# A gated state-space block: from a scheduled order of units to a written order of pairs

## The chip, the core and the metric

The kernel runs on one core of a Trainium2 chip. The core has five engines that work side by side, each on its own queue of instructions and in the order of that queue: TensorE (PE in the profile; its weight loads are shown apart as PEld), VectorE (DVE), ScalarE (ACT), GpSimd (POOL) and SyncE (SP), which here only issues DMAs. Results of TensorE land in PSUM, a small memory of eight banks; everything else is kept in SBUF, and DMAs move data between SBUF and the large memory (HBM).

The metric is the time of one execution on the device in microseconds (us). All arithmetic is in 32-bit floats.

## The reference

The input is four sequences of 512 tokens with 512 channels. A small modulation first: `mod = silu(c) @ wmod` gives six vectors of 512 for every sequence (shift, scale and gate, twice). Then

- `h = layernorm(x) * (1 + ca) + sa`, and a Mamba-2 layer on `h`: a projection to 3136 columns (1024 of x, 512 of B, 512 of C, 1024 of z, 64 of dt), a causal convolution of four taps and silu on x, B and C, `dt = softplus(...)`, the chunked scan below, a skip term, a product with `silu(z)` and a projection back to 512 columns;
- `x = x + ga * that`, a second layer norm with its own shift and scale, a 512 x 512 product with binarized weights (sign times mean size) and a bias, and `x = x + gb * that`.

The scan has 64 heads of 16 channels; eight heads share one group of B and C (64 states). In chunks of 128 tokens:

```
A_cum        = cumsum(-dt) inside the chunk
Lm[s, z]     = exp(A_cum[s] - A_cum[z])    for z <= s, else 0
Y_diag[s]    = sum_z  (C[s] . B[z]) * Lm[s, z] * X[z]
states[c+1]  = states[c] * exp(A_cum[end]) + sum_z B[z] * exp(A_cum[end] - A_cum[z]) * X[z]
Y_off[s]     = (C[s] . states[c]) * exp(A_cum[s])
y            = Y_diag + Y_off + D * X / dt
```

## The kernel before

The 2048 tokens are worked on in eight **halves** of 256 tokens (`T`), two to a sequence, each with two chunks of 128. The groups are taken two at a time (`gp`, four of them). A **unit** is one chunk of one half and one `gp`, that is 16 heads; there are 64 units, eight to a half.

For each half there is a **front**: load and layer norm (`f_norm`), transposes on TensorE and modulation into `hT` (`f_hT`), dt and its cumulative sums (`f_dt`, which writes the sums to HBM, `sums_d`, so that they can be read back repeated over 128 partitions), the tiles of 128 projected columns (`f_B`, `f_C`, `f_x` through `conv_pair`, and `f_z`; the products are `proj`, L432 to 434), and transposes of x and B to token order (`f_xt`, `f_Bt`). A convolved tile needs one ACT instruction (L450) and three DVE instructions (L454), a pair of tiles one tanh (L458) and one last DVE product (L459).

For each unit there are three stages. `stage0` loads the sums into two `decay` tiles of 128 x 8 x 128 (L541 and L542) and, except in a sequence's first chunk, the tile `e`. `stage1` masks C.B (`gm`, L621), takes eight exponentials for each decay tile on ACT (`exps`, L549) and multiplies each tile by `gm` on DVE (L625). `stage2` makes the 16 **strip** products `py` (TensorE, 32 columns of its array each, four of them side by side; L212 and L215), gathers the output on DVE and POOL (L666 to L675), and feeds the states (`new_states`). `burst` (L598) makes the products of C with B and with the states for two units at a time in the bank `gy`. There are four decay tiles, so two units have their tiles at once; for the last units, free parts of the weights `win` are used as well.

For each chunk a **tail** follows: the output projection `po` (L739), gates, layer norm, transposes `ph`, modulation `h`, the product `pf` (L775) and the store of `o`.

The order in which each engine gets its instructions isn't the order in which the Python code runs. The tables `FRONT`, `FIRST` and `SECOND` give the steps at which parts are traced, and the scheduler of the tile framework then orders the instructions from their priorities and its own estimates. The kernel bends that order in places: `glued` keeps a row of products together and places it behind the newest projection (`tc.issue_after`), `behind` places a front's later part behind the half's newest projection, `first_dt` raises the priority. Early in the run one queue, SP, carries all loads in turn: the inputs, `win`, then `load_late` (4 MB of modulation weights that borrow the place of `wout` and `bwT`), later `wout` itself (2 MB, `load_wout`) and the four 256 KB tiles `fw` of the second layer's weights (`signs`, L272, summed by DVE in L274). PSUM has five banks for everything in rotation (tag `mm`), two for `gy`, one for `py`.

Of the kernel before, what the change touches and what calls it, by code (L numbers as in the profile page):

```python
# [2 lines left out]

# [8 lines left out]
F32 = mybir.dt.float32  # L12
# [24 lines left out]
SERIES = [0.11612164612, 0.108532879004, 0.142961789972, 0.19999853166, 0.333333336603]  # L37


@with_exitstack  # L40
def adaln_mamba_block(
# [31 lines left out]
    xs_of = {}  # L73

    def load_x(h, queue=nc.sync):
# [5 lines left out]
        xs_of[h] = tiles  # L81


    ct = keep.tile([P, NK, B], F32, name="ct")
    nc.sync.dma_start(ct, cT)
    load_x(0, nc.scalar)


    ident = keep.tile([P, P], F32, name="ident")
    make_identity(nc, ident)  # L90
    ones = keep.tile([P, P], F32, name="ones")
    nc.gpsimd.memset(ones, 1.0)

    upto = keep.tile([P, P], F32, name="upto")
    nc.gpsimd.affine_select(
        out=upto, in_=ones, compare_op=ALU.is_ge, fill=0.0, base=0,
        pattern=[[1, P]], channel_multiplier=-1,
    )
    mhalf = keep.tile([P, 2], F32, name="mhalf")
    nc.gpsimd.memset(mhalf, -0.5)  # L100


    NXP = 4
    xpads = []
    for i in range(NXP):
        xp = keep.tile([P, 2, 2 * HPG * 2 * HD], F32, name=f"xpad{i}")
        xpads.append(xp)

    NE = 4
    decays = []  # L110
    for i in range(NE):
        et = keep.tile([P, HPG, CH], F32, name=f"decay{i}")
        decays.append(et)

    win = keep.tile([P, NK, PROJ], F32, name="win")
    wout = keep.tile([P, NKI, DM], F32, name="wout")
    bwT = keep.tile([P, NK, DM], F32, name="bwT")
    modT = keep.tile([P, 4, NK, B], F32, name="modT")
    gate_d = dram.tile([B, 3, DM], F32, name="gate_d")
    sums_d = dram.tile([NHALF, 2, NH, CH], F32, name="sums_d")  # L120
    e_d = dram.tile([NHALF, 2, NH, CH], F32, name="e_d")
    r_d = dram.tile([NHALF, NH, 2, CH], F32, name="r_d")

    w_in_v = w_inT.rearrange("(k p) e -> p k e", p=P)

    def load_win(lo, hi, after=None):
        d = nc.sync.dma_start(win[:, :, lo:hi], w_in_v[:, :, lo:hi])
        if after is not None:

            tc.add_manual_dep(  # L130
                d.ins, after, mybir.DependencyInfo(mybir.DependencyClass.Sync, mybir.DependencyReason.DATA)
            )
        return d.ins
# [772 lines left out]
```

## Time and profile before

| | |
|---|---|
| time, median of three executions | 737.01 us (735.02 to 738.54) |
| span of the profiled execution | 735.7 us |
| instructions | 15007 |
| TensorE busy | 700.4 us (95%) |
| VectorE busy | 599.5 us (81%) |
| ScalarE busy | 522.0 us (71%) |
| GpSimd busy | 254.8 us (35%) |
| moved by DMA | 99.24 MB, mean 135 GB/s |

The profiled execution's own time is not given apart from its span; the span lies 1.3 us below the median of the three timed executions. A line of a group reads: line, engine, operation, tile written and tiles read, shapes, how often, and behind the bar the busy time in us and the mean of one in ns, then the idle time of the engine before these instructions and what ended it. A matmul of 32-bit floats shows as two records, a transpose as one. Matmuls are pipelined: a record's duration is longer than the distance from one start to the next, and the distance is what a product costs in a row of them. In the chain of waits (the work that ended last, followed back from the end) and in the timeline, a line has start, length and what, all in us from the start of the span.

Two half-periods of the steady part: the strips of the first unit of halves 2, 3, 4, 5, 6 and 7 start at 248.4, 336.0, 421.7, 509.3, 595.0 and 682.7 us, some 86.9 us apart. Half 1 starts at 162.4 us.

### The profile page before, as it was taken

How to read it: one execution, taken by the hardware profiler on the slowest of the kernel's cores; microseconds unless marked ns; L12 is line 12 of the kernel's file. 1: busy time of each engine (PE TensorE's matmuls, PEld its weight loads, DVE VectorE, ACT ScalarE, POOL GpSimd, SP SyncE). 2: the span in 40 equal slices, each digit the busy share in tenths (PEclk: the TensorE clock that was granted, in tenths of full speed). 3: DMA queues.
4: the chain of work that ended last, by engine and by line, in shares of the span. 5: the costliest groups of instructions: out<-in, count | busy, mean ns of one | idle time of the engine just before them, and what ended most of it. 6: DMA issues, size and time to landing. Idle time of an engine off the chain costs nothing.

```text
span 735.7 us, 15007 instructions
## 1 busy us (share of the span) xinstructions
PE 700.4 (95%) x5196; PEld 500.8 (68%) x5196; DVE 599.5 (81%) x1170; ACT 522.0 (71%) x1507; POOL 254.8 (35%) x297
## 2 busy tenths in 40 slices
PE   6999979899999999999999999999999999999997
PEld 3786746666677666677677666776667866677754
DVE  3869888876998678986899768996799867996995
ACT  2467658748696697785976787865968768788941
POOL 4021323444243332343223342433414332333652
PEclk9999989999999999999999999999999999999999
DMA  8991693535555256444644256552564537457720
GB/s 279 328 291 41 204 208 85 135 98 142 127 132 144 63 155 137 102 115 102 159 116 130 53 116 168 142 137 53 140 132 114 130 86 176 116 150 151 142 69 29
DMA packets 119067, 99.24 MB, mean 135 GB/s; under 512 B 73984, under 2 KB 97152, under 8 KB 118992
## 3 DMA queue, kind: packets, MB, share of 16 engines
q1 hardware_dynamic: 117808, 96.39, 52.3%
q0 software_dynamic: 896, 1.38, 0.7%
q8 instruction: 41, 0.67, 0.4%
q10 hardware_dynamic: 288, 0.52, 0.2%
q14 instruction: 34, 0.28, 0.1%
HBM read 92.47 MB, written 5.79 MB: 134 GB/s over the span
## 4 chain that ended last, share of the span: by engine, by line
PE 65%; ACT 16%; DVE 9%; DMA 4%; issue 4%; POOL 1%; SPq 1%; ACTq 0%; DVEq 0%; POOLq 0%
PE po L739 14%; PE pp_x L434 11%; PE pp_z L434 10%; ACT decay L549 9%; PE pp_C L434 7%; PE pp_B L434 5%; PE pf L775 3%; PE py L212 2%; PE py L215 2%; DVE decay L625 2%; ACT h L759 2%; DVE u_x L454 2%; DMA fw<-in_ffn_w 2%; ACT win L549 2%; PE gy L215 2%
## 5 line engine op out<-in xcount | busy, mean ns | idle before, releaser
L549 ACT ACTIVATE decay<-decay,st 128x128 f32<-128x128 f32 x960 | 293.9, 395 | 4.2 <-DMA decay<-sums_d 3.7
L625 DVE SCALAR_TENSOR_TENSOR decay<-decay,gm 128x1024 f32<-128x1024 f32 x120 | 160.8, 1341 | 50.3 <-ACT decay L549 47.2
L434 PE MATMUL pp_x<-hT,win 128*128 128x259 f32 x512 | 120.7, 390 | 7.3 <-DVE u_C L454 7.3
L434 PE MATMUL pp_z<-hT,win 128*128 128x256 f32 x512 | 118.1, 383 | 0.0
L434 PEld LDWEIGHTS pp_x<-hT,win 128*128 128x128 f32 x512 | 96.9, 193 | 25.2 <-ACT decay L549 7.7
L739 PE MATMUL po<-wout,z 128*128 128x512 f32 x256 | 113.8, 595 | 0.0
L434 PEld LDWEIGHTS pp_z<-hT,win 128*128 128x128 f32 x512 | 94.3, 189 | 16.3 <-issue 3.5
L675 POOL TENSOR_TENSOR z<-yt,z 128x256 f32<-128x256 f32 x62 | 62.9, 1015 | 76.1 <-DVE yt L674 57.8
L454 DVE SCALAR_TENSOR_TENSOR u_x<-pp_x,cw,u_x 128x256 f32<-128x256 f32 x192 | 83.6, 474 | 1.3 <-ACT u_x L450 0.7
L739 PEld LDWEIGHTS po<-wout,z 128*128 128x128 f32 x256 | 47.5, 190 | 53.1 <-issue 52.4
L672 POOL TENSOR_TENSOR yt<-yt,xs 128x256 f32<-128x256 f32 x46 | 41.4, 899 | 106.3 <-DVE yt L671 78.6
L507 POOL TENSOR_TENSOR xs<-u_x,rr 128x512 f32<-128x512 f32 x32 | 42.7, 1334 | 79.2 <-DVE u_x L459 61.3
L516 ACT ACTIVATE uz<-pp_z,zb 128x256 f32<-128x256 f32 x64 | 27.5, 470 | 59.0 <-PE pp_z L434 59.0
L215 PE MATMUL py<-decay,xpad 128*32 128x128 f32 x1680 | 66.3, 276 | 0.0
L434 PE MATMUL pp_B<-hT,win 128*128 128x259 f32 x256 | 63.5, 396 | 2.7 <-ACT decay L549 1.9
L434 PE MATMUL pp_C<-hT,win 128*128 128x259 f32 x256 | 59.6, 384 | 1.1 <-DVE u_x L454 1.1
L775 PE MATMUL pf<-bwT,h 128*128 128x512 f32 (+1 forms) x136 | 59.0, 578 | 1.4 <-ACT h L759 1.3
L434 PEld LDWEIGHTS pp_B<-hT,win 128*128 128x128 f32 x256 | 47.4, 193 | 14.5 <-ACT decay L549 3.1
L450 ACT ACTIVATE u_x<-pp_x,cb,cw 128x256 f32<-128x256 f32 x64 | 35.3, 560 | 30.5 <-PE pp_x L434 30.4
L434 PEld LDWEIGHTS pp_C<-hT,win 128*128 128x128 f32 x256 | 47.8, 189 | 9.4 <-PE pn L424 1.4
L679 POOL TENSOR_TENSOR xd<-xpad,st 128x256 f32<-128x256 f32 x48 | 34.1, 727 | 55.8 <-PE pst L215 28.3
L212 PE MATMUL py<-decay,xpad 128*32 128x128 f32 x240 | 47.4, 279 | 3.2 <-issue 2.2
(157 smaller groups left out, 1080.9 us busy)
## 6 DMA issues: line engine op xcount, KB each, us to landing
decay<-sums_d SPq DMA_DIRECT2D x120, 256.0 KB
decay<-sums_d SPq DMA_DIRECT2D x120, 128.0 KB
rr<-r_d SPq DMA_DIRECT2D x64, 128.0 KB
e<-e_d SPq DMA_DIRECT2D x96, 64.0 KB
win<-in_w_inT SPq DMA_DIRECT2D x4, 1024.0 KB
xr<-in_x SPq DMA_DIRECT2D x16, 256.0 KB
res<-o SPq DMA_DIRECT2D x15, 256.0 KB
x<-in_x SPq DMA_DIRECT2D x14, 256.0 KB
```

The lines of the kernel that those rows point to most:

```text
L212: first = products[0]()
L215: product()
L434: last = mm(pm, win[:, k, col : col + P], H[h]["hT"][:, k, lo:], start=(k == 0), stop=(k == NK - 1))
L450: nc.scalar.activation(u[:, j, :], pm[:, KS - 1 :], AF.Identity, bias=cb[:, t : t + 1], scale=cw[:, t, KS - 1 : KS])
L454: nc.vector.scalar_tensor_tensor(u[:, j, :], pm[:, k : k + T], cw[:, t, k : k + 1], u[:, j, :], ALU.mult, ALU.add)
L507: nc.gpsimd.tensor_tensor(xs, xc, rr, ALU.mult)
L549: nc.scalar.activation(ets[r][:, i, :], ets[r][:, i, :], AF.Exp, bias=H[h]["st"][:, hd : hd + 1], scale=-1.0)
L625: nc.vector.scalar_tensor_tensor(ets[r], ets[r], 1.0, bc_mid(gm[:, r, :], HPG), ALU.min, ALU.mult)
L672: ew.tensor_add(t, t, xs)
L675: ew.tensor_mul(zg, t, zg)
L739: last_po = mm(po, H[h]["z"][g // 2][:, g % 2, c * CH : (c + 1) * CH], wout[:, g, :], start=(g == 0), stop=(g == NKI - 1))
L775: mm(pf, h2[:, k, :], bwT[:, k, cols], start=(k == 0), stop=(k == NK - 1))
```

## The change

Tile's scheduler is no longer asked for the order: the whole body runs inside `tc.manual_schedule()`, and each engine issues in the order in which the code traces its instructions. That order comes from a small queue. Every part of the work is a Python generator (a task) that yields the planned time of its next piece; `Plan.run` always continues the task with the smallest planned time. The planned times are in a table `PLAN`, in units of one step (eight to a half), with own rows for the first half (`@0`) and the last (`@7`). `glued`, `behind`, `first_dt` and all `issue_after` are gone.

The scan works on **pairs** of units: 32 pairs in place of 64 units. `gm`, `e`, `yt`, `py`, `z` and `xs` are tiles for a pair, so the DVE and POOL instructions on them have 512 elements in a row of a partition where they had 256, and there are half as many. The 32 strip products of a pair are traced in one block. There are six decay tiles (`ND`), four to a pair, in rotation: of the next pair's four tiles, two can be loaded before this pair's strips are done. To make room in SBUF, the scratch memory for DMA descriptors is cut to 2048 bytes (`SCRATCH`).

Smaller edits: `new_states` makes eight products of 32 columns in place of four of 64; `f_Bt` turns only the first chunk in a sequence's second half (two transposes in place of four, in four halves); the signs of the second layer's weights are made in place; `load_late` is planned at -3.55, ahead of all loads of decay tiles (-2.85 and later) and of `rr`, while before its first load stood ahead of them and the other five behind the first four decay tiles; `wout` is planned at 1.25 and the first `fw` load at 2.3.

```diff
+class Plan:
+    def at(self, t, f, *args):
+        self.push(t, f(*args))
+    def push(self, t, task):
+        heappush(self.queue, (t, self.count, task))
+        self.count += 1
+    def run(self):
+        while self.queue:
+            now, _, task = heappop(self.queue)
+            t = next(task, None)
+            if t is not None:
+                self.push(max(now, t), task)
...
+TAP = 0.04
+ND = 6
+PLAN = {
...
+    "loads": (-3.55, 1.25,),
+    "signs0": (2.3, 2.7, 1.95, 2.85, 3.25, 3.4,),
...
+    "B0": (1.15, 1.3, 1.4, 1.55, 1.75, 1.85,),
...
+    "pair1": (2.0, 0.1, 0.5, 1.2, 1.65, 2.1, 2.1, 2.35, 2.4, 2.65, 2.3, 2.35, 2.5,),
+    "decay10": (-0.95, -0.6, -0.2, 0.2,),
+    "decay11": (0.1, 1.05, 1.2, 1.6,),
...
+    "decay02@0": (-2.6, -1.8, -1.3, -0.85,),
+    "decay03@0": (-2.85, -1.5, -1.0, -0.75,),
...
-    def glued(products, after=None):
-        with tc.issue_after(after) if after else nullcontext():
-            first = products[0]()
-        with tc.issue_after(first.ins), tc.high_priority(offset=1000):
-            for product in products[1:]:
-                product()
...
+    def f_Bt(h, q, w):
+        n = 1 if h % HPB == HPB - 1 else 2
+        pt = to_tokens(H[h]["B"][q], f"bt_{h}_{q}", n)
...
+    def decayed(n, i, room, w):
+        h, c, q = of_pair(n)
...
+        et = rooms[room]
...
+        nc.sync.dma_start(et[0:mid], src.partition_broadcast(mid))
+        nc.sync.dma_start(et[mid:, :, mid:], src[:, mid:].partition_broadcast(mid))
+        for k in range(HPG):
+            yield w[1] + (w[2] - w[1]) * k / (HPG - 1)
+            hd = c * NH + head + k
+            nc.scalar.activation(et[:, k, :], et[:, k, :], AF.Exp, bias=H[h]["st"][:, hd : hd + 1], scale=-1.0)
+        yield w[3]
+        gm = gm_of[n]
+        nc.vector.scalar_tensor_tensor(et, et, 1.0, bc_mid(gm[:, i % 2, i // 2, :], HPG), ALU.min, ALU.mult)
...
+    def masked(n):
...
+        gm = wk.tile([P, 2, 2, CH], F32, tag="gm", name=f"gm_{n}", bufs=1)
+        nc.vector.tensor_mul(gm, new_of[n], upto.unsqueeze(1).unsqueeze(1).to_broadcast([P, 2, 2, CH]))
...
+    def strips(n, w):
+        h, c, q = of_pair(n)
+        py = ps.tile([P, 2, 2, CH], F32, tag="y", bufs=1, name=f"py_{n}")
+        for u in range(2):
+            xp = xp_of[h, 2 * q + u][:, c, :]
+            for r in range(2):
+                et = decay_of[n, 2 * u + r]
+                for s in range(2):
+                    for j in range(HPG // 2):
+                        lo = r * 2 * P + 32 * (2 * j + s)
+                        mm(
+                            py[32 * j : 32 * j + 32, r, u, :], xp[:, lo : lo + 32], et[:, 2 * j + s, :],
+                            start=(s == 0), stop=(s == 1),
+                        )
...
+            for j in range(4):
+                mm(pst[32 * j : 32 * j + 32, u, :], bt[:, c, u, 32 * j : 32 * j + 32],
+                   xd[:, j // 2 * P : (j // 2 + 1) * P], start=True, stop=True)
...
+                room = ND + 4 * (n % 2) + i if n >= NPAIR - 2 else (4 * n + i) % ND
+                w = planned(f"decay{p}{i}", h, now)
+                at(w[0], decayed, n, i, room, w)
...
+    with tc.manual_schedule():
+        plan.run()
...
-    nc = bacc.Bacc("TRN2", target_bir_lowering=False, num_devices=1)
+    nc = bacc.Bacc("TRN2", target_bir_lowering=False, num_devices=1, dynamic_dma_scratch_size=SCRATCH)
```

Laid out in the order of issue on TensorE, the block of strips of a pair, its `gy` burst and its `pst` products now mostly stand next to each other; before, the strips stood in 72 places and the dt products `pa` in 22, now in 32 and 8.

## The prediction

> **What bounds the kernel now.** I read the spans and busy shares first, then the chain of waits, then TensorE's own waits, then the timeline of a steady stretch.
>
> ```profile
> core 0: 735.7 us, clock 0.993
> ...
> PE 700.4 (95%) x5196; PEld 500.8 (68%) x5196; DVE 599.5 (81%) x1170; ACT 522.0 (71%) x1507; POOL 254.8 (35%) x297
> ...
> PE 65%; ACT 16%; DVE 9%; DMA 4%; issue 4%; POOL 1%; SPq 1%; ACTq 0%; DVEq 0%; POOLq 0%
> ```
>
> TensorE is the bound, but busy time says little, since pipelined records overlap. The chain of waits gives the true price of a product in a row of them:
>
> ```profile
> 357.56 3.70 PE pp_B L434 x16
> 361.27 3.51 PE pp_C L434 x16
> 364.77 6.87 PE po L739 x16
> 371.64 0.30 PE gy L212
> ```
>
> A 259-column product costs 3.51/16 = 0.219 us, a 512-column one 6.87/16 = 0.429. The first row is the same work as the second and 0.19 longer: before it TensorE stood on the narrow products `py` and `pa` and had to change to another tile of its array. The other direction is in the timeline:
>
> ```profile
> 341.00 0.60 PE L757 MATMUL ph<-ident,t 128*128 128x128 f32 x4
> 341.53 0.30 PE L212 MATMUL py<-decay,xpad 128*32 128x128 f32 x1
> ...
> 346.78 0.37 PE L212 MATMUL gy<-C,S 64*128 64x128 f32 x1
> 346.79 0.37 PE L215 MATMUL gy<-C,S 64*128 64x128 f32 x1
> 347.00 0.27 PE L212 MATMUL gy<-C,S 64*128 64x128 f32 x1
> ```
>
> Four transposes cost 4 x 0.109 = 0.44, but `py` starts 0.53 after them: 0.09 for the change. The second step of `gy` follows after 0.22 and the later ones after 0.112: 0.11 more. So a change of tile form costs 0.1 to 0.2 us; over all 247 changes in the trace the mean is 0.17.
>
> The sum of TensorE's time, then. Products in a row: 1024 x 0.219 + 512 x 0.216 (`pp_z`) + 256 x 0.429 (`po`) + 120 x 0.429 and 16 x 0.215 (`pf`) = 500; strips 512 groups of four x 0.109 = 56; `gy` 224 x 0.112 = 25; transposes 372 x 0.109 = 41; the rest (`pst`, `pa`, `pg`, `pn`) 26: together 648. Changes of form: 247 x 0.17 = 42. First product at 6.2, and 4.0 from the start of the last one to the end. What is left of 735.7 is 735.7 - 648 - 42 - 10.2 = 35.5: true waits. Where they lie:
>
> ```profile
> PE pp_x L434 <- DVE u_C L454: 7.3, 2, 5.4
> PE pg L221 <- DVE sc L197: 6.2, 1, 6.2
> PE pa L368 <- ACT hT L347: 3.3, 8, 0.6
> ```
>
> ```profile
> 83.06 13.38 DMA fw<-in_ffn_w
> ...
> 99.41 6.23 PE pp_x L434 x16
> ```
>
> ```profile
> 90.00:97.60 7.60, 3.93 (x51) 2.84 (x49) 5.80 (x17) 3.51 (x8) 4.31 (x7) 1.00 1.11 239
> 97.60:104.50 6.90, 5.09 (x12) 4.08 (x13) 6.90 (x16) 4.70 (x14) 0.95 (x2) 0.51 1.06 256
> ```
>
> The longest (5.4 us, the first row) is the `fw` load behind 2 MB of `wout`: DVE waits for it in L274, its convolution taps stand behind, five banks of PSUM fill, TensorE stops. The last table (busy time of PE, PEld, DVE, ACT, POOL, then clock) shows the price again: 6.9 us at clock 0.51, some 3.4 lost. With 1.7 lost at another half-clock stretch near 16 us and smaller gaps before 140 us, the start has 19.5 of the 35.5; the end 3.2; the steady part 12.8, about 1.9 for each half.
>
> **The change, part by part.**
>
> *Fewer changes of form.* In the written order of each kernel I count them: 247 before, 134 after (strips stand in 32 places in place of 72, `pa` in 8 in place of 22, `pst` next to narrow work). 113 x 0.17 = 19.2 off the path. Bounds: 0.09 (the entry alone) gives 10, 0.20 gives 23. I take the mean of the whole trace.
>
> *Products.* 16 transposes fewer: 16 x 0.109 = 1.7 off. `pst` has eight products of 32 columns where it had four of 64. No row shows `pst` so; side by side as `py` is (four in 0.109) they take the same two steps, one by one 96 steps more x 0.109 = 10. I take 0, since `py`, the same tile form, starts its four 7 ns apart.
>
> *DVE and POOL.* 176 DVE instructions of 256 elements (L621, L666, L671, L674; 0.41 each) become 88 of 512 (0.69, as L742): 72 - 61 = 11 less. On POOL 108 of 0.90 to 1.02 become 54 (1.33, as L507): 32 less. I cost both at nothing: TensorE covers them.
>
> *Two of four decay tiles are late.* With six tiles, two of the next pair's can be loaded only after this pair's strips. The path: load 3.9 to 5.0 (the chain's rows `decay<-sums_d`), two tiles of exponentials 2 x 2.44, one mask 1.24: about 11. In the shortest interval between two pairs TensorE has 16 `pp` products of each of two kinds (7.0), `po` (6.9), strips (1.75), `pt_bt` and `gy` (0.9), changes (0.5) = 17.0, so 15.2 after the strips. Adding each engine's rows between the same marks, DVE has 15.9 and ACT 14.5 there; in the longest interval 27.8, 23.2 and 19.8. TensorE has the most work in every steady interval, so I cost this wait at 0; without that cover it would be about 1 us a pair.
>
> *The start.* The `fw` loads are planned a step after `wout` (some 11 us), so I let the 5.4 and its 3.4 of clock go. What is late next: `load_late` now stands ahead of the first decay tiles on SP, 3.1 MB more than before. At 287 GB/s (mean of the first 60 us) that is up to 10.7 us; the first exponentials, at 46.3 before, come between 46 and 57. TensorE's written order gives it products until about 59 (16 tiles of 1.75, three z of 3.5 and 6 of small work after 16.75, less the 2 of `pa` that lie before); ACT has some 19 to do there: 40 exponentials (0.305 each, 12), eight taps and tanhs (7). If the loads land at 46 and the taps and tanhs fall beside them, the strips are ready by 59: no wait. If they land at 57 and all 19 comes after: 76, a wait of 17. I take 7, a little under the middle, because the first tile to land already feeds ACT. Start: 1.7 + 7.3 of small gaps + 7 = 16.
>
> *Order as written.* All queues are now strict as traced, and a wait at the head of ACT, DVE, POOL or SP holds what is planned behind it: exponentials hold convolution taps and so PSUM banks; on SP a store of `o` (L907) holds decay loads. POOL's own four DMAs a half stand behind its `xd` and ahead of `z`; three steps pass before `sums_d` is read. Bounds for the steady part: 0, and 25 (twice the present 12.8, from the idle of a queue that passes on its waits). Of the present ones, those of `pa` and `phT` among split strips (0.5 to 0.9 each) go; I take 10. The end keeps its chain `po`, norm, `ph`, `pf`: 4.
>
> *Sum.* 6.2 + (648 - 1.7) + 134 x 0.17 (22.8) + (16 + 10 + 4) + 4.0 = 709.3 of span. The span before lies 1.3 under its median; that gives 710.6, and I say 710.
>
> **A rule weighed.** The row: a gap of 5.4 us was followed by 6.9 us at clock 0.51; one of 2.1 us near 130 was not (clock 1.00 from 128 to 132). The Trainium skill, "TensorE: Matmul & The Clock Gate", section "HAM oscillation — how this bites in real kernels", puts the limit at gaps of about 3.4 us. By the rows a gap between 2.1 and 5.4 is undecided, and 7 would be a fall of the clock if it came in one piece; my sum assumes that it comes in several and stays at 710. By the page's limit one piece of 3.4 is enough, and with it the sum would be about 714.
> The same page, in "Architectural detail: the array is 16× 32×32, not 1× 128×128", calls the ACT and DVE queues strict first-in first-out, which speaks against a finely interleaved written order; this trace has 214 us of idle ACT and passes only a few us on to TensorE.
>
> **The rivals.**
>
> 1. *Nearly all waits vanish.* For it: TensorE has the most work in each interval. Against: the loads at the start. Waits 9 + 0 + 3 = 12: 691 + 1.3 = 692. Chance 0.20 (below 700).
> 2. *The start gets worse:* the first strips wait 17 in one piece with 3.4 of clock, and `fw` is late again (5.4): 10 + 3.4 + 5.4 = 19 over my sum: 729. For it: the DMA share is 0.93 in the first 60 us, so nothing comes early. Chance 0.17 (718 to 734).
> 3. *The change doesn't do what it says:* the time for changes of form only moves into waits for operands, 19 + 7 back: 736, within 0.5% (734 to 741). Chance 0.05.
> 4. *Slower: every pair waits for its last two decay tiles.* The place is `strips`: 32 products in one block, so `pst` and the projections stand behind the fourth mask on TensorE, where before eight strips could go with one tile. For it: ACT has 14.5 of the 17.0 us between pairs and its exponentials stand in line with taps that wait for TensorE. Against: 15.2 us of cover for 11. It decides from 1.0 us a pair (31 pairs, 31 us over my sum); at 1.6 a pair 50 more: 760. Chance 0.16.
>
> My own case (700 to 718) has 0.42. Faster by over 0.5% is 0.42 + 0.20 + 0.17 = 0.79, within 0.5% (about what a measurement of this kernel can tell from none) 0.05, slower 0.16. The range that leaves out two in ten, some 0.06 below and 0.14 above: 691 to 742.
>
> **What would show it.** Right: `pp_B` and `pp_C` in the chain mostly at 3.51; halves 82 to 84 us apart in place of 86.9; TensorE's longest waits below 5 us and before 75 us; no clock of 0.5 near 100 us. Wrong: `py` waiting for DVE `decay` or ACT in every pair (rival 4); `fw` or `decay` loads again at the start of the chain (rival 2); halves still near 87 with few waits on TensorE (the price of a change mis-sized). The forecast fails if in-order waits exceed 60 us in all.

## The result and the profile after

| | before | after |
|---|---|---|
| median time | 735.03 us (20 executions, 732.98 to 738.54) | 739.97 us (20 executions, 735.19 to 745.91) |
| ratio after to before, 95% interval | | 1.0068 [1.0047, 1.0089] |
| span of the profiled execution | 735.7 us | 742.7 us (its time is 744.44) |
| mean granted clock of TensorE | 0.993 | 0.978 |

The change makes the kernel 0.7% slower. The forecast was 710 us, with a range of 691 to 742. The profiled execution lies 4.5 us above the median of its kernel; the accounts below are made against its own span.

These lines answer to those of the prediction. The spans:

```profile
core 0: 742.7 us, clock 0.978
```

The page's busy times, and the shares of the chain that ended last:

```profile
PE 690.0 (93%) x5372; PEld 506.9 (68%) x5372; DVE 606.1 (82%) x1080; ACT 523.5 (70%) x1507; POOL 239.3 (32%) x245
...
PE 44%; DVE 22%; DMA 12%; ACT 12%; issue 5%; SPq 3%; POOL 1%; ACTq 0%; DVEq 0%; POOLq 0%
```

TensorE held 65% of that chain before and holds 44% now; DVE went from 9 to 22% and DMAs from 4 to 12%. Less of the chain is TensorE's own work, and more of it is work that TensorE waited for. Part of the chain around a pair's strips (start, length, what):

```profile
610.13 3.51 PE pp_C L563 x16
...
614.28 1.88 PE py L771 x64
616.16 0.44 PE pst L824 x16
616.60 3.65 PE pp_z L563 x16
```

`pp_C` costs 3.51 here, since it stands behind `pp_B` of the same form; `pp_z` behind the narrow `pst` costs 3.65 for 16 x 0.216 = 3.46, a change of 0.19. All strips of a pair stand in one block of 1.88 us. `pst` takes 0.44 for its 16 records, 0.027 each, like the strips: the eight narrower products cost nothing more, as was assumed.

TensorE's largest groups of waits, from the list of what each engine waited for (us in total, times, longest); the row left out (`pg`, 6.5 us at the very start) has its like in the kernel before:

```profile
PE ph L885 <- DVE t L437: 12.2, 2, 8.4
PE py L771 <- ACT decay L707: 7.3, 4, 3.0
...
PE py L771 <- DVE decay L710: 4.4, 2, 2.4
PE pt_bt L621 <- DVE B L572: 3.9, 5, 1.5
PE gy L717 <- DVE C L572: 3.4, 1, 3.4
```

**Where the time is, by stage.** For each stage I take TensorE's time from one start to the next, subtract the products at the prices of the prediction and the changes of tile form (247 before at 0.17 us; 134 after, at 0.178 from this trace), and call the rest waits; what a lowered clock costs is in them.

| TensorE, us | changes before | changes after | waits before | waits forecast | waits after |
|---|---|---|---|---|---|
| up to the first strips of half 1 | 8.2 | 5.0 | 18.5 | 16 | 20.4 |
| from there to the first strips of half 7 | 30.4 | 17.1 | 12.8 | 10 | 20.8 |
| the rest | 3.4 | 1.8 | 0 | 4 | 17.3 |
| sum | 42.0 | 23.9 | 31.3 | 30 | 58.5 |

18 us of changes are off, and 27 us of waits have come. (For the kernel before this account finds 31.3 us of waits where the prediction's sum left 35.5; the prices leave some 4 us over in either kernel.) Against the forecast, the waits are 58.5 - 30 = 28.5 of the 33.4 us between its span (709.3) and the measured one; changes are 1.1 more, and the other 4 are what the prices leave over.

By marks it reads so: the strips of half 1 start 6.2 us sooner than before (156.2 for 162.4), the next six halves take 513.6 in place of 520.3, so half 7's strips start 12.9 sooner (669.8 for 682.7). 3.9 us of that are work that now stands behind the mark (16 records of `pp_x`, 3.5, and four transposes, 0.4), so the real lead is 9.0. Then comes the end: 72.9 us in place of 53.0.

One trace of a kernel is one execution. The steady stretch of six halves, 513.6 us here, takes 507.9 to 512.3 us in the traces of seven kernels below that have the same steady plan; the end takes 73.6 and 73.9 us in the two that have the same end.

TensorE in the end of the changed kernel, from the timeline (start, length, what, and in brackets the idle time before and what ended it):

```profile
702.41 0.71 PE L717 MATMUL gy<-C,S 64*128 64x128 f32 x8 [0.84 <-DVE yt L781]
711.50 1.12 PE L885 MATMUL ph<-ident,t 128*128 128x128 f32 x4 [8.38 <-DVE t L437]
712.55 3.64 PE L771 MATMUL py<-win,xpad 128*32 128x128 f32 x64
...
731.05 1.12 PE L885 MATMUL ph<-ident,t 128*128 128x128 f32 x4 [3.85 <-DVE t L437]
```

The last block of strips takes 3.64 us where a block takes 1.88 to 1.95. The table by windows says why (busy times of PE, PEld, DVE, ACT, POOL, then the granted clock, the DMA share and GB/s):

```profile
584.10:590.90 6.80, 6.27 (x44) 5.04 (x45) 6.13 (x15) 0.63 (x1) 2.50 (x3) 0.50 0.79 184
...
706.90:717.20 10.30, 5.70 (x70) 4.26 (x71) 7.08 (x11) 4.95 (x16) 3.76 (x2) 0.50 0.00 0
...
730.80:737.70 6.90, 5.77 (x15) 4.47 (x16) 0.92 (x3) 1.50 (x4) 1.26 (x1) 0.51 0.01 4
```

With each of TensorE's four waits of 3 us and more (3.4 at 67.6, 3.1 at 584.6, 8.4 at 711.5, 3.9 at 731.1) its clock falls to a half, for 6.8 or 10.2 us. Over the span 16.2 us of clock are lost so in the changed kernel and 5.1 in the kernel before. Part of each half-clock stretch lies inside the wait itself and costs nothing more; counted only where TensorE is busy, 11.2 us are lost, and 4.2 before.

ACT in the same end. These are the exponentials of the last two pairs, whose tiles lie in `win`:

```profile
691.32 8.89 ACT L707 ACTIVATE win<-win,st 128x128 f32<-128x128 f32 x30 [1.19 <-DMA win<-sums_d]
701.77 8.58 ACT L707 ACTIVATE win<-win,st 128x128 f32<-128x128 f32 x29 [1.56 <-DMA win<-sums_d]
```

Both rows start when a load has landed. The loads themselves stood on SP behind a store of `o`, which waited for DVE until 686.07.

### The profile page after: what moved, and what is told of

It is laid out like the page before. It is cut to its first block, busy times and chain, and to the rows that moved or that the text cites. A ratio compares the mean times of both kernels' runs of the same rounds, so it can differ in the third digit from the quotient of the medians.

```text
span 742.7 us, 15145 instructions
## 1 busy us (share of the span) xinstructions
PE 690.0 (93%) x5372; PEld 506.9 (68%) x5372; DVE 606.1 (82%) x1080; ACT 523.5 (70%) x1507; POOL 239.3 (32%) x245
## 4 chain that ended last, share of the span: by engine, by line
PE 44%; DVE 22%; DMA 12%; ACT 12%; issue 5%; SPq 3%; POOL 1%; ACTq 0%; DVEq 0%; POOLq 0%
PE pp_z L563 9%; PE po L867 9%; DMA decay<-sums_d 7%; ACT decay L707 7%; DVE u_x L581 6%; DVE decay L710 5%; PE pp_B L563 4%; PE pp_x L563 4%; PE py L771 4%; PE pp_C L563 3%; PE pf L901 3%; DMA x<-in_x 2%; DVE u_B L581 2%; PE gy L717 2%; DMA rr<-r_d 1%
## 5 line engine op out<-in xcount | busy, mean ns | idle before, releaser
L707 ACT ACTIVATE decay<-decay,st 128x128 f32<-128x128 f32 x960 | 305.1, 390 | 40.7 <-DMA decay<-sums_d 36.8
L563 PEld LDWEIGHTS pp_x<-hT,win 128*128 128x128 f32 x512 | 95.5, 192 | 21.9 <-issue 6.1
L581 DVE SCALAR_TENSOR_TENSOR u_x<-pp_x,cw,u_x 128x256 f32<-128x256 f32 x192 | 88.6, 481 | 14.4 <-ACT u_x L576 11.0
L771 PE MATMUL py<-decay,xpad 128*32 128x128 f32 x1920 | 62.1, 280 | 12.3 <-ACT decay L707 7.3
L771 PEld LDWEIGHTS py<-decay,xpad 128*32 128x32 f32 x1920 | 52.0, 112 | 17.6 <-ACT decay L707 8.2
L563 PE MATMUL pp_B<-hT,win 128*128 128x259 f32 x256 | 60.5, 383 | 0.9 <-issue 0.9
L581 DVE SCALAR_TENSOR_TENSOR u_C<-pp_C,cw,u_C 128x256 f32<-128x256 f32 x96 | 45.5, 481 | 19.2 <-ACT u_C L576 17.4
L793 POOL TENSOR_TENSOR yt<-yt,xs 128x512 f32<-128x512 f32 x23 | 37.9, 1650 | 52.9 <-DVE yt L791 52.8
L581 DVE SCALAR_TENSOR_TENSOR u_B<-pp_B,cw,u_B 128x256 f32<-128x256 f32 x96 | 45.4, 481 | 8.8 <-ACT u_B L576 7.2
L433 POOL TENSOR_TENSOR rs_f<-rs_f,mhalf 128x1 f32<-128x1 f32 x16 | 11.7, 733 | 121.9 <-DVE rs_f L432 121.9
L797 POOL TENSOR_TENSOR z<-yt,z 128x512 f32<-128x512 f32 x31 | 43.9, 1415 | 14.6 <-DVE yt L795 11.3
```

What stands on the lines that cost most here:

```text
L433: nc.gpsimd.tensor_tensor(rs, rs, mhalf[:, :n], ALU.pow)
L563: mm(pm, win[:, k, col : col + P], H[h]["hT"][:, k, lo:], start=(k == 0), stop=(k == NK - 1))
L581: nc.vector.scalar_tensor_tensor(u, pm[:, k : k + T], cw[:, tile_, k : k + 1], u, ALU.mult, ALU.add)
L707: nc.scalar.activation(et[:, k, :], et[:, k, :], AF.Exp, bias=H[h]["st"][:, hd : hd + 1], scale=-1.0)
L771: mm(py[32 * j : 32 * j + 32, r, u, :], xp[:, lo : lo + 32], et[:, 2 * j + s, :], start=(s == 0), stop=(s == 1),)
L793: ew.tensor_add(yt, yt, xs)
```

## The experiments

My theory after reading this was that nothing in the pair-wide structure costs the time, but the written order does: (1) in the steady halves SP stands at stores of `o` and holds the loads behind them; (2) the end is ordered so that ACT is late and the norms lie open; (3) each long wait costs as much again in clock. The rivals: the saving of 19 us was never there; the first loads cost it; or ACT, DVE and POOL have no slack left, so that a wait taken away comes back elsewhere. The last half's pairs are 28 to 31; tail (7, 0) and tail (7, 1) belong to its two chunks. Times are medians, to be read against 739.97 for the changed kernel; "x [a, b]" is the ratio to the kernel before on the same chip.

### What a change of tile form costs

```
         for q in range(2):
             proj(pm[:, q, :], h, NCONV + (2 * j + q) * P, KS - 1)
+            if q == 0:
+                mm(pm[0:32, 1, 0:CH], win[:, 0, NCONV : NCONV + 32],
+                   H[h]["hT"][:, 0, KS - 1 : KS - 1 + CH], start=True, stop=True)
```

> One narrow product (32 columns of weights, 128 x 128) is put between the two gate projections of each `z` tile; its result is written over by the second projection and used by nothing. That is 32 more narrow products of 0.1 us and 64 more changes between wide and narrow. If a change of form costs what the sum of the prediction took (0.17 us in the mean), TensorE gets 64 x 0.17 + 32 x 0.1 = 14 us more and the kernel is 10 to 14 us slower (some of it in waits that exist anyway): 750 to 754. If a change of form costs nothing by itself (the saving of the change was never there), it is the 32 products' 3 us or less: 740 to 743.

Measured: 751.32 us, 11.4 over the changed kernel, 1.0218 [1.0199, 1.0237]. The same stretch of the timeline, first in the changed kernel, then here:

```profile
282.95 3.72 PE L563 MATMUL pp_z<-hT,win 128*128 128x256 f32 x16
286.61 0.71 PE L717 MATMUL gy<-C,S 64*128 64x128 f32 x8
```

```profile
285.61 2.00 PE L563 MATMUL pp_z<-hT,win 128*128 128x256 f32 x8
287.53 0.41 PE L667 MATMUL pp_z<-hT,win 128*32 128x128 f32 x2
287.87 2.00 PE L563 MATMUL pp_z<-hT,win 128*128 128x256 f32 x8
289.80 0.71 PE L720 MATMUL gy<-C,S 64*128 64x128 f32 x8
```

From `pp_z` to `gy` it is 3.66 us there and 4.19 here. The product shows as two records, which at 0.109 take 0.22; the other 0.31 are two changes, 0.155 each. The price of the prediction (0.17, bounds 0.1 to 0.2) holds, and so does the saving. (32 x 0.53 = 17 us of work were put in and 11.4 show; that the rest went into waits that exist anyway is not shown.) The rival "the saving was never there" falls.

### The stores on SP

```
             nc.vector.tensor_add(o, o, x2[:, cols])
+            if parts == 1:
+                yield w[11] + 0.8
             nc.sync.dma_start(out[...], o)
```

> The store of `o` (L907) is written 0.8 of a planned step later, so that the sum that it waits for is over when SP reaches it. Theory A (the stores hold SP, and with it the loads of `rr`, `x` and the decay sums behind them): the changed kernel has 182 us of SP waiting for `o` in 16 waits, and its matmuls wait 7.3 us for decay (ACT) and 4.4 us for masks (DVE) in halves 1 to 6; with the store later, SP's wait for `o` falls under 60 us, those two waits fall under 4 us in all, and the time falls by 6 to 12 us, to 728 to 734. Theory B (the loads behind the stores have slack enough, the waits come from the order on ACT and DVE): the time stays within 3 us of 740 and the two waits stay above 8 us.

Measured: 734.0 us, 6.0 below the changed kernel, 0.9975 [0.9955, 0.9995]. In the changed kernel, SP's queue and TensorE around 560 us:

```profile
560.68 0.35 SPq L907 DMA_DIRECT2D res<-o  x1
561.20 2.58 SPq L643 DMA_DIRECT2D rr<-r_d  x4
563.83 0.93 SPq L249 DMA_DIRECT2D x<-in_x  x2
564.86 0.49 SPq L702 DMA_DIRECT2D decay<-sums_d  x1
```

```profile
584.63 1.08 PE L771 MATMUL py<-decay,xpad 128*32 128x128 f32 x16 [3.05 <-ACT decay L707]
```

SP had issued its last load at 553.14 and then waited 7 us for the store's operand; four loads of `rr`, two of `x` and then the decay loads came behind it, and the fourth tile of the next pair was 3.05 us late. A clock of 0.50 (the first row of the windows above) followed. With the store later, the list of SP's waits has these rows (L909 and L249 are the store and the load behind it):

```profile
SPq L909 <- DVE o L906: 89.0, 8, 22.1
SPq L249 <- DVE o L906: 28.9, 6, 9.8
```

118 us together in place of 182, more than the 60 that I expected; but in the steady halves `py` waits 0.3 us in place of 7.3, and ACT waits 6.7 us for decay loads in place of 23.3. (The 4.4 us for masks, which I had placed in halves 1 to 6, stand in half 0, and are 5.6 now.) The six halves from the strips of half 1 to those of half 7 take 501.8 us in place of 513.6, with 9.0 us of waits left of 20.8. A fairer measure takes all traces: 501.8, 503.2 and 503.8 with the later store, 507.9 to 513.6 in eight kernels without it whose steady plan is else the same, some 7 us apart in the mean, which agrees with the 6.0 of the medians. The store's place cost that much of the steady part. The end did not move: 73.6 us.

### The first loads

```
-    "loads": (-3.55, 1.25,),
+    "loads": (-1.45, 1.25,),
```

> The loads of the late modulation weights (`load_late`) are written at -1.45 instead of -3.55, behind the first decay loads of half 0 on SP. Theory A (these big loads hold the first decay tiles up and so the first strips, 70.6 us in the changed kernel): the first strips start 3 to 8 us sooner and the time falls by 2 to 8 us, to 732 to 738. Theory B (the first strips wait for ACT and DVE work of half 0, not for loads): the first strips stay within 2 us of 70.6 and the time within 2 us of 740.

Measured: 741.17 us, 1.0082 [1.0052, 1.0112]. The first strips start at 73.2 (70.6 in the changed kernel), and `gy` waits 9.8 us in place of 3.4 for the last DVE product of `C`. So neither theory's numbers come. Why `C` is late can be read from the chain of waits and from ACT's own waits between 40 and 75 us, first in the changed kernel, then here:

```profile
ACT decay L707 <- DMA decay<-sums_d: 7.4, 3, 3.5
...
54.13 7.06 DMA decay<-sums_d
...
66.04 0.52 ACT th_C L570
```

```profile
ACT decay L707 <- DMA decay<-sums_d: 9.6, 1, 9.6
...
50.62 13.08 DMA decay<-sums_d
...
68.56 0.52 ACT th_C L570
```

The tanh of `C` (`th_C`) stands behind exponentials on ACT, and these wait for decay loads: 7.4 us in three waits in the changed kernel, 9.6 in one wait here. The first exponentials did come sooner (45.3 us in place of 48.3), but the moved loads now stand ahead of the next decay tiles, and one of those takes 13.1 us to land. So the loads are in the chain of either kernel; this edit only moved their place, and doesn't show what the first strips would cost without `load_late`. As the reason why the kernel is slower than before, the start is too small all the same: it has 20.4 us of waits for 18.5.

### The end: three tries

Loads and exponentials of pairs 30 and 31 earlier, and pair 30 waiting for the projections of B and C alone:

```
-            for lo in range(0, NCONV, P):
+            for lo in range(DI, NCONV, P) if n == NPAIR - 2 else range(0, DI, P):
...
-    "decay20@7": (1.55, 2.0, 2.15, 2.35,),
+    "decay20@7": (-1.3, -0.6, 0.9, 2.35,),
...
-    "decay30@7": (2.75, 3.15, 3.65, 3.65,),
+    "decay30@7": (0.65, 1.6, 2.5, 3.65,),
```

> Only the last half is changed: the loads and exponentials of the last four units (pairs 30 and 31) are planned 1.3 to 4 steps earlier, and pair 30's tiles, which lie on the columns of `win` of B and C, wait for those projections alone. Theory A (the end loses its time because ACT's last exponentials come late: strips of half 7 begin at 669.8 us of 742.7, 72.9 us before the end, against 53.0 in the kernel before): the end shrinks to 53 to 62 us and the time to 727 to 733. Theory B (the end is bound by the tails after the last strips: DVE's masks, norms and the last output products, whatever ACT does): the end stays above 68 us and the time at 736 to 742.

Measured: 756.0 us, 1.0271 [1.0237, 1.0304]: slower by 16. On SP the early loads now stand in front of pair 29's first one, which pair 28's exponentials are mixed with on ACT; ACT stood 6.2 us for it, and TensorE in the middle of pair 28's strips:

```profile
675.13 1.08 PE L771 MATMUL py<-decay,xpad 128*32 128x128 f32 x16 [5.61 <-ACT u_x L576]
```

"Earlier" in a strict order is always earlier than something else. The second try put the loads behind that one and wrote the whole last half anew (strips, bursts, masks and both tails; only the rows of exponentials and tails are shown):

```
+    "decay20@7": (-0.9, 0.0, 0.4, 2.4,),
+    "decay21@7": (-0.85, 0.1, 0.5, 2.45,),
...
+    "tail0@7": (1.55, 2.7, 3.05, 3.15, 3.2, 3.25, 3.45, 3.48, 3.7, 3.75, 4.2, 4.7, 4.75,),
+    "tail1@7": (2.2, 3.5, 4.0, 4.3, 4.35, 4.4, 4.6, 4.65, 5.0, 5.05, 5.2, 5.5, 5.55,),
```

> The last half's plan is written anew, and nothing else: the loads of pair 30's tiles go out behind those of pair 29's second and not before, their exponentials fill ACT's gaps at 670 to 678, those of pair 31 follow 8 to 10 us sooner than in the changed kernel; bursts, masks, strips and the two tails are laid so that a product stands beside each gating and norm. Theory A (the end loses 20 us through its order alone: late exponentials on ACT, `ph` waiting 8.4 us behind masks, an uncovered norm of 3.9, an uncovered gating): the last 72.9 us become 56 to 62 and the time 725 to 732. Theory B (pair-wide strips can't be packed at the end: all 32 exponentials, 4 masks and a whole gating must be over before the next product, whatever the order): the end stays above 68 us and the time above 735. The earlier attempt (loads in front of pair 29's) speaks for B if this fails too.

Measured: 739.45 us, 1.0062 [1.0036, 1.0088]: nothing won. After the last strips the kernel now needs 20.5 us in place of 30.2, but those strips start at 721.3 in place of 712.5. The reason is again on ACT and then TensorE:

```profile
673.40 4.77 ACT L709 ACTIVATE win<-win,st 128x128 f32<-128x128 f32 x16
```

```profile
688.97 0.82 PE L623 MATMUL pt_xt<-ident,u_x 128*128 128x128 f32 x4 [4.77 <-DVE u_x L574]
```

16 exponentials of pair 30 ran ahead of the conv work of the last `x` tile, which pair 29 needs: 4.77 us on ACT, 4.77 us of wait on TensorE.

A smaller step, alone: `pf` of tail (7,0) behind `po` of tail (7,1), where it lies beside the last norm.

```
+    "tail0@7": (1.55, 2.7, 3.05, 3.45, 3.5, 3.6, 3.8, 3.9, 4.35, 4.45, 5.4, 6.1, 6.1,),
```

> One thing is moved: the feed-forward product `pf` of tail (7,0) is written behind the last output product `po` of tail (7,1) instead of ahead of it, so that its 3.6 us of TensorE lie beside the last norm. In the changed kernel TensorE waits 3.85 us for that norm (ph L885 at 731.05). Theory A (work that used to cover the norms stands at the wrong place): that wait falls to under 1 us and the time by 2.5 to 4.5 us, to 735.5 to 737.5. Theory B (the end is set by when the last exponentials on ACT are over, and TensorE has nothing else that it could do): the time stays within 2 us of 740.

Measured: 734.1 us, 0.9991 [0.9967, 1.0015], 5.9 below the changed kernel. TensorE:

```profile
705.34 1.12 PE L886 MATMUL ph<-ident,t 128*128 128x128 f32 x4 [8.31 <-DVE t L438]
...
721.64 0.66 PE L886 MATMUL ph<-ident,t 128*128 128x128 f32 x4 [0.42 <-DVE t L438]
```

The wait of 3.85 is 0.42 now, and the half clock that followed it is gone, so that more came back (5.9 us by the medians) than the wait; the wait of 8.3 is still there. From half 7's strips to the end it is 67.5 us in place of 72.9.

The third try mends the second: only pair 30's first tile goes ahead (into 2.8 us in which ACT is idle), and strips 31 stand ahead of `po` of tail (7,1).

```
+    "decay20@7": (-0.9, -0.12, -0.06, 2.4,),
+    "decay21@7": (-0.85, 0.71, 0.89, 2.45,),
+    "decay22@7": (-0.8, 1.46, 1.7, 2.55,),
...
+    "pair3@7": (3.5, 3.19, 2.1, 3.95, 3.95, 3.6, 3.7, 3.8, 3.85, 3.9, 4.65, 4.7, 4.35,),
```

> The last half's plan again, mended where the first new plan failed: there ACT ran 16 exponentials of pair 30 (4.8 us) in front of the conv work of the last `x` tile, and strips 29 came 7 us late (695.8 for 688.6), and half of `po` stood in front of strips 31. Now only the first tile of pair 30 goes ahead, into ACT's idle 2.8 us at 670; strips 31 stand ahead of `po` of tail (7,1), and `pf` of tail (7,0) behind it. Theory A (order alone loses the end): strips 29 stay at 18 to 19 us behind strips 28, strips 31 come 36 to 38 us behind strips 28 (42.7 in the changed kernel), the end after strips 31 takes 20 to 24 us (30.2), and the time is 725 to 731. Theory B (a pair-wide end can't be packed, whatever the order): the end behind strips 28 stays above 68 us and the time above 735.

Measured: 739.15 us, 1.0038 [1.0013, 1.0063], by its median no gain. Its profiled execution took 733.67, 5.5 below that median, so its trace can't show what the median lost. In that trace strips 29 start 19.2 us behind half 7's first (strips 28), the last strips 43.7 us behind them, and the end follows 26.8 later: 70.5 in all. Theory A's numbers are missed in each place, and theory B's are met.

### Both together

The later store with the second plan of the end, and with the third:

> The later store (which took 6 us) and the new plan of the last half in one kernel. If the two losses are separate (steady halves and end), their gains add: 740 - 6 - 11 = 723, between 717 and 727, which is below the kernel before (735). If the end waits for ACT and the steady part's gain makes ACT late by as much, the gains don't add: 728 to 734.

Measured: 733.5 us, 0.9972 [0.9952, 0.9992].

> The later store (which took 6 us alone) with the mended plan of the last half. If the losses are separate, 740 - 6 - 12 = 722, between 718 and 726, below the kernel before (735). If the end is bound by ACT alone, the steady halves' gain is given back: 728 to 732.

Measured: 732.76 us, 0.9954 [0.9934, 0.9974]. Both are faster than the kernel before, and both gain only what the store gains alone. The rewritten end adds 0.5 and 1.2 us to it, not the 11 and 12 expected.

### The clock, by itself

Products that nothing reads, ahead of `ph` in both tails of the last half. First 18 and 8 of them, then 9 and 4:

```
+        if h == NHALF - 1:
+            pd = ps.tile([P, DM], F32, tag="mm", name=f"pd_{c}")
+            for _ in range(4 if c else 9):
+                mm(pd, ident, bwT[:, 0, :], start=True, stop=True)
```

> The changed kernel with products that nothing reads put into TensorE's two long waits at the end: 18 of 128 x 512 (7.7 us) ahead of `ph` of tail (7,0), 8 (3.4 us) ahead of `ph` of tail (7,1). In the changed kernel the granted clock is a half from 706 to 718 and from 730 to 738, after these waits, and 8.5 us are lost so. Theory A (the waits themselves make the clock fall): with TensorE kept busy the clock stays at 1.0 in the last 40 us, the strips and products there run in 1.8 and 3.6 us in place of 3.6 and 4.2 to 6, and the time falls by 3 to 7 us, to 733 to 737, although TensorE has more to do. Theory B (the half clock has another cause, or the work is not bound by TensorE there): the time stays within 2 us of 740 or rises.

Measured: 743.65 us, 1.0109 [1.0093, 1.0125]. I had forgotten that each product shows as two records and costs 0.86: the fill was 22.8 us of work in place of 12.2 us of waits. The clock stayed at 1.00 through the end, and although TensorE had 10.5 us more to do than it had waited, the time rose by only 3.7. Half as many:

> The changed kernel with unread products in TensorE's two waits at the end again, half as many: each of them was issued as two, so that the first try gave TensorE 15.7 and 7.0 us of work in place of waits of 8.4 and 3.9. Now 9 and 4 products stand there, 7.9 and 3.5 us. In the first try the clock stayed at 1.0 through the last 45 us. Theory A (a waiting TensorE loses its clock, and the products after the wait pay for it): half 7's strips start 72.9 us before the end in the changed kernel and 77.8 in the first try; with the fill sized to the waits this falls to 65 to 68, and the time to 732 to 736. Theory B (the clock is not what was lost, the chain of ACT and DVE is): it stays above 71 and the time within 2 us of 740.

Measured: 736.84 us, 1.0034 [1.0009, 1.0059], 3.1 below the changed kernel and 0.8 above the range expected. The windows of the end:

```profile
695.50:706.00 10.50, 9.60 (x46) 4.65 (x50) 7.65 (x11) 8.65 (x30) 4.43 (x4) 1.00 0.07 20
706.00:717.00 11.00, 11.00 (x82) 5.58 (x71) 4.15 (x7) 1.22 (x4) 1.24 (x1) 1.00 0.07 25
717.00:730.00 13.00, 8.84 (x31) 5.08 (x29) 4.66 (x10) 1.50 (x4) 1.82 (x2) 1.00 0.06 21
```

Half 7's strips start 67.3 us before the end in place of 72.9, and the last block of strips takes 1.95 us in place of 3.64. With useless work in the gap, the useful work behind it runs at full clock. That is shown: a long wait of TensorE costs its own length, and then, in the changed kernel, 2.4 to 3.1 us of clock on the work behind it. That the whole kernel became faster is likely and not certain: 3.1 us by the medians, but the executions overlap (732.63 to 742.23 against 735.19 to 745.91).

### Can the structure be had below 722 by moving planned times?

More planned times moved, on top of the later store and the third plan of the end:

```
-    "z3@0": (0.55, 0.9, 1.0, 1.15,),
+    "z3@0": (-0.1, 0.9, 1.0, 1.15,),
-    "Bt1": (6.3, 6.15,),
+    "Bt1": (6.6, 6.62,),
+    "decay22@0": (2.12, 2.65, 3.05, 3.0,),
+    "decay23@0": (2.13, 3.25, 3.45, 3.65,),
...
+    "decay22@7": (-0.8, 1.66, 1.8, 2.55,),
+    "pair2@7": (3.0, 2.0, 2.05, 2.5, 3.5, 3.18, 3.2, 3.25, 3.26, 3.28, 3.25, 2.7, 3.1,),
+    "pair3@7": (3.5, 3.01, 2.1, 3.95, 3.95, 3.6, 3.7, 3.8, 3.85, 3.9, 4.65, 4.7, 4.35,),
+    "tail0@7": (1.55, 2.7, 3.05, 3.3, 3.31, 3.32, 3.4, 3.45, 3.74, 3.76, 4.2, 4.7, 4.75,),
```

> Planned times alone again, on top of the later store and the last half's second plan: the transposes of the second `B` tile stand behind the second `C` projection (they waited 1.0 us in each of 7 halves), the last gate projection of half 0 ahead of the first strips (TensorE waited 3.9 + 1.9 us there), two decay loads of pair 2 ahead of a wait on SP (a mask came 4.2 us late), and at the end pair 30's last exponentials behind the gate work and pair 31's mask product earlier (TensorE waited 4.0 + 2.5 + 2.0 us). Theory A (the change's structure has the time that was forecast; its table of planned times loses it): most of the 20 us of waits and 5 of clock that these places hold go, and the time is 710 to 722. Theory B (ACT and DVE bind in place of TensorE as soon as waits are taken away): the time stays above 727.

Measured: 729.31 us, 0.9922 [0.99, 0.9945]. It is the fastest version here: 10.7 us below the changed kernel, 6.3 below the kernel before, and 7 above what theory A asked for. The end takes 65.1 us now (72.9, and 53.0 before). From 125 to 655 us TensorE's list of waits has just these:

```profile
PE po L871 <- POOL z L801: 8.6, 7, 1.5
PE pp_z L567 <- ACT xpad L656: 1.4, 6, 0.2
```

The 7.2 us of waits for `B` that this kernel had before the edit (in 7 halves) are gone, and 8.6 us for POOL's gating stand in their place: `po` came sooner, and its operand didn't. So the last edit moved half of that `po` behind the next projection (and put `z3@0` back):

```
-    "z3@0": (-0.1, 0.9, 1.0, 1.15,),
+    "z3@0": (0.55, 0.9, 1.0, 1.15,),
-    "tail1": (5.5, 6.7, 7.05, 7.45, 7.55, 7.6, 7.8, 7.9, 8.35, 8.45, 8.95, 9.35, 9.45,),
+    "tail1": (5.5, 6.7, 7.4, 7.65, 7.7, 7.72, 7.85, 7.9, 8.35, 8.45, 8.95, 9.35, 9.45,),
```

> The last mended kernel with two of its places changed: `po` of each half's second tail has its second half behind the next `x` projection (in the mended kernel it waited 0.5 to 1.5 us for POOL's gating in 7 halves, 8.6 us in all, which had taken the place of 7.2 us of waits of the `B` transposes), and the last gate projection of half 0 goes back behind the first strips (ahead of them, it moved the wait of 3.7 us to the transposes behind it and the strips from 68.4 to 70.8). Theory A (each of these waits is one of order, and they go one by one): 729.3 - 8 - 3 = 718, between 714 and 723. Theory B (a wait that is taken from TensorE comes back at the next place, since POOL, DVE and ACT have no slack): 726 to 732.

Measured: 732.37 us, 0.9962 [0.9949, 0.9975], 3.1 above the mended kernel. The waits for POOL are gone from the steady halves, and these are the longest there now:

```profile
PE phT L470 <- DVE x L441: 4.4, 6, 0.9
PE pt_xt L625 <- DVE u_x L576: 2.6, 9, 0.5
PE py L775 <- issue: 2.5, 4, 0.8
```

By the account by stage (as above) the waits of the six halves are 20.8 us in the changed kernel, 9.0 with the later store, 11.9 in the mended kernel and 18.0 in this one. They fell to 9 by one edit and not below it by any other, where one and the same plan can differ by 6 us from trace to trace. Theory A holds for the store and for `pf`; for the last 9 to 12 us of the steady part and most of the end, theory B fits better: in the changed kernel DVE is busy for 445 of the 514 us of those halves (87%), and a wait taken from TensorE there came back behind another engine. That DVE is the cause is argued and not shown; no run gave it less work.

## Why the prediction was wrong, point by point

**Changes of form: right.** 134 are in the trace, and TensorE's time for them fell from 42.0 to 23.9 us, where 22.8 were forecast. The extra changes put in cost 0.155 us each, inside the bounds. **Products, `pst`: right**, as the row of 0.44 us shows.

**Late decay tiles (rival 4): right to leave out.** `py` waits for ACT and DVE 6 times in all, 11.7 us together, and not 1 us or more in every one of 31 pairs. The strips of most pairs find their tiles ready, and with the later store the steady ones nearly all do (0.3 us).

**DVE and POOL costed at nothing: right in what was counted, wrong as room.** The four kinds of DVE work that became wide fell from 71.3 to 60.1 us (`gm` 26.1 to 21.9, `yt` 45.2 to 38.2), the 11 less that was worked out. But the convolution's taps, the same work, went from 170.7 to 179.5 us of busy time, although one takes 474 ns before and 481 after: they overlap less. DVE is busy for 606.1 us in place of 599.5; POOL has 15 less, not 32. That DVE, at 82% in a strict order, has hardly any room to be late is argued and not shown.

**The start: near in its size, its cause partly open.** 16 forecast, 20.4 found. (The sum's 7.3 of small gaps should be 9.0, what 19.5 leaves after 5.4, 3.4 and 1.7; with it the start is 17.7.) The stall on `fw` is gone as foretold: no half clock near 100 us. The first strips wait 3.4 us for `C` and 2.4 for a mask, 5.7 together where 7 were taken; the clock behind both (half from 68.7 to 75.5 us, 2.4 lost) was not in the sum. Both waits stand behind exponentials that wait for decay loads, as the sum had it. That `load_late` is what holds these loads up is not shown: the one run that moved it put it ahead of other decay loads.

**Order as written, steady part: the first step that failed.** I took 10 us between bounds of 0 and 25, and named the store of `o` on SP as one way. It was the main one: 20.8 us were found, and 9.0 with the store alone written later (15 to 21 in the eight traces of this steady plan, 9 to 11 in the three with the later store). The value inside the bounds was chosen with the hope that the waits of split strips would go; the row to choose by was SP's own idle time before its stores, 27.0 us in 10 waits before, which grew to 181.7 in 16.

**"The end keeps its chain: 4" is the step that failed most.** 17.3 us were found. I looked at the chain of products (`po`, norm, `ph`, `pf`) and not at what stands beside it. Before, the last strips are eight blocks, of which the last leaves only 8 of the 16 records of `po` (1.98 and 1.88 us), and `pf` (3.6) lies beside the norm; the norm's wait is 0.42. After, a whole pair is the last block; 29 of its 32 exponentials come in one piece behind one load, its masks follow, then all 16 records of `po` (7.03), and nothing lies beside the norm, whose wait is 3.85. Then the clock adds to each wait. One edit to that order (`pf`) gave back 5.9 us.

**The rule on the clock: it should have been in the sum.** I let 10 us of waits be short pieces that leave the clock alone. Counted where TensorE is busy, 7 us more clock were lost than before. (By that count the half clock near 100 us cost 2.5 us before, not the 3.4 of the sum; and the gap near 130 us that I weighed is 1.9 us in TensorE's list, not 2.1.) The Trainium skill, "TensorE: Matmul & The Clock Gate", section "HAM oscillation — how this bites in real kernels", warns of gaps over about 3.4 us. The rows here agree for the gaps of 8.38 and 3.85, and go further: a gap of 3.05 came with the half clock too. In the fifteen traces of this case, all 37 gaps of 3.05 us and more behind the first product come with it, at the latest 1.4 us after their end, and it lasts 3.4 to 13.7 us. Of the shorter ones some do (2.35 in the first try at the end, 2.87 in the third) and some don't (2.46 and 2.59 in the second try, 2.55 with half the fill). In the mended kernel three gaps of 1.37 to 1.56 within 6.5 us were enough. The second row below is the clock that followed:

```profile
695.00:701.50 6.50, 2.62 (x68) 1.72 (x56) 5.73 (x4) 1.81 (x7) 4.31 (x2) 1.00 0.01 4
701.50:708.50 7.00, 6.37 (x37) 3.04 (x38) 6.06 (x11) 0.00 (x0) 1.81 (x2) 0.52 0.00 0
```

TensorE was busy for 2.62 of 6.5 us there. Below 3 us the length of one gap does not decide it in these traces; that it is how little TensorE did in some microseconds fits these rows, and no run tests it by itself.

**The rivals.** Rival 3 (a chance of 0.05) named the number, 734 to 741, and the account: the time for changes moves into waits. It did: 18 us of changes went and 27 of waits came. But its mechanism is not a law of this structure: moving planned times brought the kernel to 729.31, 0.8% below the kernel before. How much of the remaining 19 us to the forecast can be had is open; the last edit of the table did not give any of it.

## What to carry to other kernels

When a scheduler's order is replaced by a written one, cost every queue's head: an instruction that waits holds all that is planned behind it, most of all a store on a queue that also carries loads. Make the account of the end by itself: what is the last block of work, how long must the engines before it run for it, and what lies beside each norm and each gating. And give each wait of the matrix engine of 3 us and more, and several shorter ones close together, its price in clock; here that price, counted where TensorE is busy, was 11.2 us in the changed kernel, beside four such waits of 18.6 us in all.

## What was not expected of the hardware

DVE and POOL slow each other when both work on tiles in SBUF. In the mended kernel a mask of 128 x 1024 takes 1.21 to 1.23 us wherever no POOL instruction runs beside it (67 masks). Of the four in the first row below, the first and the last take 1.21, and the two that start while a POOL instruction runs take 2.29 each:

```profile
696.38 6.77 DVE L714 SCALAR_TENSOR_TENSOR win<-win,gm 128x1024 f32<-128x1024 f32 x4
```

```profile
696.54 2.18 POOL L797 TENSOR_TENSOR yt<-yt,xs 128x512 f32<-128x512 f32 x1 [6.50 <-DVE yt L795]
698.80 2.13 POOL L801 TENSOR_TENSOR z<-yt,z 128x512 f32<-128x512 f32 x1
```

The POOL instructions take 2.18 and 2.13 us in place of 1.27. The Trainium skill, "SBUF — State Buffer", section "SBUF: two separate sides", says that the two engines share a pair of ports that one of them holds for a whole instruction while the other waits. These rows agree: the four slowed instructions take 0.9 or 1.1 us more than alone, a little less than what was left of the other engine's instruction when they started (1.0 to 1.2 us). It matters here because masks and gating are the last things before the strips and before `po`.

The other surprise is how far one program's executions spread: 735.19 to 745.91 for the changed kernel in 20 executions, 732.98 to 738.54 for the one before in as many. That TensorE's many waits are the reason is a guess; no run tests it, and the mended kernel's four executions (728.43 to 731.64) are too few to tell.
